# A two-layer relational graph network: gathers of the first six chunks, layer 1's weight sums and the buffers of gathered rows are moved

## The chip, the core and the metric

The kernel runs on one NeuronCore of one Trainium2 chip. The metric is the device time of one execution in microseconds. Before the change it is 22033.58 us, the median of three runs (22026.26, 22033.58, 22033.65). The execution that the profiler recorded took less: 16730.85 us, of which the trace covers 16729.1 us. The page does not say why the two differ; all times of single stages below are times of the recorded execution.

## What is computed

There are 50,000 nodes with 128 features each and 850,000 edges, sorted by the node they point to (`dst`). Each edge has a source node `src` and one of 16 relation types. Two layers run one after the other, the second on the output of the first, and the input is added and normalised at the end:

```python
W = jnp.einsum('rb,bio->rio', w_comp, basis)          # 16 relations from 8 bases, 128x128 each
seg = dst.astype(jnp.int32) * N_REL + rel.astype(jnp.int32)
agg = jax.ops.segment_sum(h[src], seg, num_segments=N_ENT * N_REL)
msg = jnp.einsum('nri,rio->no', agg.reshape(N_ENT, N_REL, -1), W)
out = relu(msg + h @ loop_w + bias)
...
x = _layernorm(x + layer2(layer1(x)), axis=-1)
```

Everything is float32. The costly part of the data movement is `h[src]`: 850,000 rows of 512 bytes per layer, from arbitrary places.

## The kernel before

The edges are cut into tiles of 128, and ten tiles (`K = 10`) make a chunk; there are 665 chunks (`C`) per layer, 1,330 in all. The work has two parts, with a branch between them.

**The part ahead of the branch** (lines 151 to 293) turns the edge list into tables that stay in SBUF: `src` (the row numbers, one column of 128 for each tile), `key` (relation and slot of each edge), `slot`, `dist` and `base_i` (where each chunk's nodes lie). It works in seven batches (line 232). A batch loads `raw` through the SyncE queue (line 240, two buffers), VectorE derives `own` and `rel0` from it (lines 261 to 279), ScalarE casts the row numbers (line 281), TensorE transposes both (line 287), and ScalarE and VectorE copy the results into `src` and `key` (line 288). A batch covers 8 groups of 120 tiles, so the first one holds the row numbers of the first 96 chunks. The last value, `good` (line 293), says whether the edges are sorted closely enough for the fast way. Each engine loads it (line 568) and branches.

**The part behind the branch** is `chunked()` (line 316), unrolled for all chunks of both layers. It begins with `combine(0)`, the weights of layer 1. For each relation, VectorE multiplies one base by a coefficient (line 128) and adds seven more (line 130): 128 instructions of 128x128 for a layer, inputs and output all in SBUF. `combine(1)`, layer 2's weights, stands behind layer 1's chunks in the source. The kernel language's scheduler is free to issue an instruction earlier than it stands in the source where nothing it depends on forbids it.

For each chunk, GpSimd issues ten indirect DMAs (`gather`, line 296), each fetching 128 rows into one slice of a buffer `g` out of the pool `gp`, which has six buffers. VectorE builds `hot`, a one-hot matrix of the ten tiles (line 392). TensorE multiplies each gathered tile by it (line 403), two tiles to a PSUM bank `pa` out of the pool `ps_a` (three banks), and ScalarE copies each bank to `aT` (line 410). `finish` for the chunk before is called behind the first two banks: sixteen matmuls with the weights (line 335), then the sums over shared nodes (lines 347 and 351), the loop term (line 355) and the output (lines 357 to 369).

A gather waits for the buffer it writes, and through the semaphores that the kernel language hands out, for the gather eight before it. The buffer comes free when the ten matmuls of the chunk six before have read it. The scheduler puts the wait for this on the first gather of a chunk only. Where a gather needs two waits, the first becomes a wait instruction of its own on GpSimd's queue: the built program has 1,330 of these for 13,282 gathers.

Two operands of VectorE, `grid` and `apart`, are kept in PSUM (lines 93 to 100), so that `hot` and `shift` each have one input in SBUF.

Of the kernel before, what the change touches and what calls it, by code (L numbers as in the profile page):

```python
# [26 lines left out]
F32 = mybir.dt.float32  # L27
# [4 lines left out]
OP = mybir.AluOpType  # L32
# [4 lines left out]
P = 128  # L37
# [3 lines left out]
K = P // WN  # L41
S = K * WN
G = P // K * K
BATCH = 8
EPS = 1e-5
BANK = 512

# [6 lines left out]
def tile_rgcn_resnorm(  # L54
# [15 lines left out]
    nc = tc.nc  # L70
    N, D = x.shape
    NR, NB = w_comp1.shape
    E = edges.shape[1] // 3
    n_tiles = -(-E // P)
    C = -(-n_tiles // K)
# [8 lines left out]
    consts = ctx.enter_context(tc.tile_pool(name="consts", bufs=1))  # L84
# [36 lines left out]
        BIAS.append(b)  # L121
        W.append(consts.tile([P, NR, D], F32, name=f"w{n}"))

    def combine(n):

        for r in range(NR):
            w = W[n][:, r, :]
            nc.vector.tensor_scalar(w, BASIS[n][:, 0, :], COMP[n][:, r, 0:1], None, op0=OP.mult)
            for b in range(1, NB):
                nc.vector.scalar_tensor_tensor(  # L130
                    w, BASIS[n][:, b, :], COMP[n][:, r, b : b + 1], w, op0=OP.mult, op1=OP.add
                )

    ps_a = ctx.enter_context(tc.tile_pool(name="ps_a", bufs=3, space=PSUM))
    ps_o = ctx.enter_context(tc.tile_pool(name="ps_o", bufs=1, space=PSUM))
    ps_n = ctx.enter_context(tc.tile_pool(name="ps_n", bufs=1, space=PSUM))

    def turned(h, m, sb):

# [6 lines left out]
    def column(j, first, ap):  # L146

        return bass.AP(tensor=edges.tensor, offset=edges.offset + j * E + first, ap=ap)


    n_groups = -(-n_tiles // G)
# [7 lines left out]
    with tc.tile_pool(name="meta1", bufs=1) as m1, tc.tile_pool(name="meta", bufs=2) as mp:  # L159
# [34 lines left out]
        for c0 in range(0, C, D):  # L194
            cs = slice(c0, min(c0 + D, C))
            k = cs.stop - c0
# [35 lines left out]
        for i in range(n_batches):  # L232
            g0 = i * BATCH
            q = min(BATCH, n_groups - g0)
            t0 = g0 * G
            raw = mp.tile([P, 3, BATCH, P], I32, name="raw")
            whole = min(q, (E // P - t0) // G)
            for j in range(3):
                if whole:
                    nc.sync.dma_start(  # L240
                        raw[:G, j, :whole, :], column(j, t0 * P, [[P, G], [G * P, whole], [1, P]])
                    )
            if whole < q:

                nc.vector.memset(raw[:, 0, whole, :], 0)
                nc.vector.memset(raw[:, 1, whole, :], N)
                nc.vector.memset(raw[:, 2, whole, :], NR)
                t1 = t0 + whole * G
                n_whole, n_rest = divmod(E - t1 * P, P)
                for j in range(3):  # L250
                    if n_whole:
                        nc.sync.dma_start(
                            raw[:n_whole, j, whole, :], column(j, t1 * P, [[P, n_whole], [1, P]])
                        )
                    if n_rest:
                        nc.sync.dma_start(
                            raw[n_whole : n_whole + 1, j, whole, :n_rest],
                            column(j, (t1 + n_whole) * P, [[n_rest, 1], [1, n_rest]]),
                        )
            tb = mp.tile([P, BATCH], F32, name="tb")  # L260
            nc.vector.tensor_scalar(tb[:G, :q], raw[:G, 1, :q, 0], float(N - WN), None, op0=OP.min)
            rel0 = mp.tile([P, BATCH, P], F32, name="rel0")
            nc.vector.tensor_tensor(  # L263
                rel0[:G, :q], raw[:G, 1, :q, :], tb[:G, :q, None].to_broadcast([G, q, P]), op=OP.subtract
            )
            own = mp.tile([P, BATCH, P], F32, name="own")
            nc.vector.tensor_scalar(own[:G, :q], rel0[:G, :q], 0.0, None, op0=OP.is_ge)
            nc.vector.scalar_tensor_tensor(
                own[:G, :q].rearrange("p g e -> p (g e)"),
                rel0[:G, :q].rearrange("p g e -> p (g e)"),  # L270
                float(WN),
                own[:G, :q].rearrange("p g e -> p (g e)"),
                op0=OP.is_lt,
                op1=OP.mult,
                accum_out=picked[:G, i : i + 1],
            )
            nc.vector.scalar_tensor_tensor(  # L277
                rel0[:G, :q], raw[:G, 2, :q, :], float(WN), rel0[:G, :q], op0=OP.mult, op1=OP.add
            )
            srcf = mp.tile([P, BATCH, P], F32, name="srcf")  # L280
            nc.scalar.copy(srcf[:G, :q], raw[:G, 0, :q, :])
            for of, to, engine in ((srcf, src, nc.scalar.copy), (rel0, key, nc.vector.tensor_copy)):
                for h0 in range(0, q, BANK // P):
                    h = min(BANK // P, q - h0)
                    tp = ps_a.tile([P, BANK], F32, name="pa")
                    for j in range(h):
                        nc.tensor.transpose(tp[:, j * G : (j + 1) * G], of[:G, h0 + j, :], ident[:G, :G])  # L287
                    engine(to[:, (g0 + h0) * G : (g0 + h0 + h) * G], tp[:, : h * G])
        pick = m1.tile([P, 1], F32, name="pick")
        nc.vector.tensor_reduce(pick, picked, AX.X, OP.add)  # L290
        total = ps_o.tile([P, D], F32, name="po")
        nc.tensor.matmul(total[:1, :1], pick, ones[:, 0:1], start=True, stop=True)
        nc.vector.tensor_scalar(good, total[:1, :1], float(E + C + S * C), None, op0=OP.is_equal)

    def gather(to, of, idx):
        nc.gpsimd.indirect_dma_start(  # L296
            out=to, out_offset=None, in_=of, in_offset=bass.IndirectOffsetOnAxis(ap=idx, axis=0)
        )

    def normed(t, m, sb):  # L300

# [12 lines left out]
        return o  # L314

    def chunked():
        combine(0)
        with tc.tile_pool(name="gp", bufs=6) as gp, tc.tile_pool(name="hp", bufs=2) as hp, tc.tile_pool(
            name="sb", bufs=3
        ) as sb:  # L320

# [49 lines left out]
            for n, of in enumerate((x, H1)):  # L371
                kept, late = None, None

                def finish(kept, c, k, aT, hw, n0, xw):
                    kept, a = nodes_of(c, k, slots(c, k, aT, n), kept, hw, n)
                    ended(n, a, n0, xw)
                    return kept

                for c in range(C):
                    ks = min(K, n_tiles - c * K)  # L380
                    n0 = at(c)
                    hw = sb.tile([P, D], F32, name="hw")
                    nc.sync.dma_start(hw, of[ds(n0, P), :])
                    xw = None
                    if n:
                        xw = sb.tile([P, D], F32, name="xw")
                        nc.sync.dma_start(xw, x[ds(n0, P), :])
                    g = gp.tile([P, K, D], F32, name="g")
                    for k in range(ks):
                        gather(g[:, k, :], of, src[:, c * K + k : c * K + k + 1])  # L390
                    hot = hp.tile([P, K, NR * WN], F32, name="hot")
                    nc.vector.tensor_tensor(  # L392
                        hot[:, :ks],
                        grid[:, None, :].to_broadcast([P, ks, NR * WN]),
                        key[:, c * K : c * K + ks, None].to_broadcast([P, ks, NR * WN]),
                        op=OP.is_equal,
                    )
                    aT = hp.tile([P, NR, S], F32, name="aT")
                    for k in range(0, ks, 2):
                        m = min(2, ks - k)  # L400
                        pa = ps_a.tile([P, BANK], F32, name="pa")
                        for i in range(m):
                            nc.tensor.matmul(  # L403
                                pa[:, i * NR * WN : (i + 1) * NR * WN],
                                g[:, k + i, :],
                                hot[:, k + i, :],
                                start=True,
                                stop=True,
                            )
                        nc.scalar.copy(  # L410
                            aT[:, :, k * WN : (k + m) * WN].rearrange("p r (i w) -> p i r w", w=WN),
                            pa[:, : m * NR * WN].rearrange("p (i r w) -> p i r w", i=m, w=WN),
                        )
                        if k == 2 and late is not None:
                            kept = finish(kept, *late)
                            late = None
                    if late is not None:
                        kept = finish(kept, *late)
                    late = c, ks, aT, hw, n0, xw
                finish(kept, *late)  # L420
                if n == 0:
                    combine(1)
# [189 lines left out]
```

## Time and profile before

| | busy us | share of the span | instructions |
|---|---|---|---|
| TensorE matmul (PE) | 13415.4 | 80% | 78570 |
| TensorE weight load (PEld) | 11315.1 | 68% | 78570 |
| VectorE (DVE) | 5048.0 | 30% | 10325 |
| ScalarE (ACT) | 4657.3 | 28% | 12650 |
| GpSimd (POOL) | 12558.5 | 75% | 13290 |

[...] Between two gathers the trace shows 0.30 us in which it is not busy and waits for nothing that the profile names ("issue"); a share of 75% can therefore be a queue without any hole in it. [...] The packets of all DMA queues together take 24% of the sixteen engines' time. The mean clock granted to TensorE is 0.89; its records switch between full and half.

### The profile page before, as it was taken

The numbers are of one execution on the slowest core, as the hardware profiler recorded it, in microseconds if no ns is written. First come the engines' busy times: TensorE is split into PE (matmuls) and PEld (weight loads), VectorE is DVE, ScalarE is ACT, GpSimd is POOL, SyncE is SP. The second block draws the span as 40 slices with busy tenths as digits, with TensorE's granted clock in tenths as the row PEclk, the third lists the DMA queues.
The fourth block names the chain that finished last, engine by engine and source line by source line (L and its number), as shares of the span: only waits on it lengthen the run. The fifth ranks groups of instructions, "written<-read, shape, count | busy, mean of one in ns | idle before, by whom it ended". The sixth has DMA issues, their size and how long they took to land.

```text
span 16729.1 us, 222138 instructions
## 1 busy us (share of the span) xinstructions
PE 13415.4 (80%) x78570; PEld 11315.1 (68%) x78570; DVE 5048.0 (30%) x10325; ACT 4657.3 (28%) x12650; POOL 12558.5 (75%) x13290
## 2 busy tenths in 40 slices
PE   6888888878888888888888888888878888888787
PEld 5666666666666666666666666666666666666666
DVE  4222222222222222222233333333333333333333
ACT  2222222222222222222223222222222222222222
POOL 6777777777777777777777777777777777777777
PEclk9888888888888888888888889898888888888888
DMA  3222222222222222222222222222222222222222
GB/s 75 64 64 64 64 64 64 64 64 64 64 64 64 64 64 64 64 64 64 64 66 69 69 69 69 69 69 69 69 69 69 69 69 69 69 69 69 69 69 66
DMA packets 934787, 1115.38 MB, mean 67 GB/s; under 512 B 272843, under 2 KB 721179, under 8 KB 933691
## 3 DMA queue, kind: packets, MB, share of 16 engines
q0 software_dynamic: 425024, 871.30, 18.4%
q1 hardware_dynamic: 505723, 228.35, 4.9%
q8 instruction: 649, 10.63, 0.3%
q14 instruction: 447, 3.66, 0.1%
q10 hardware_dynamic: 2944, 1.44, 0.0%
HBM read 1012.86 MB, written 87.16 MB: 66 GB/s over the span
## 4 chain that ended last, share of the span: by engine, by line
POOL 41%; PE 26%; DMA 17%; issue 16%; DVE 0%; POOLq 0%; ACT 0%; SPq 0%; DVEq 0%; ACTq 0%
POOL g L296 41%; PE ps L335 16%; DMA g<-H,src 8%; DMA g<-in_x_dram,src 8%; PE pa L403 6%; PE pn L347 1%; PE pn L351 1%; PE po L355 1%; PE po L141 0%; DMA raw<-in_edges_dram 0%; DMA first_i<-in_edges_dram 0%; POOLq L296 0%; PE pa L287 0%; DVE rel L263 0%; DVE rel L277 0%
## 5 line engine op out<-in xcount | busy, mean ns | idle before, releaser
L403 PE MATMUL pa<-hot,g 128*128 128x192 f32 x26564 | 6758.5, 367 | 3246.0 <-DMA g<-in_x_dram,src 1430.2
L296 POOL DMA_INDIRECT g<-in_x_dram,src x6641 | 6291.7, 947 | 2109.0 <-issue 1782.5
L296 POOL DMA_INDIRECT g<-H,src x6641 | 6265.8, 944 | 2039.9 <-issue 1781.9
L403 PEld LDWEIGHTS pa<-hot,g 128*128 128x128 f32 x26564 | 4307.9, 199 | 5052.1 <-ACT aT L410 1885.8
L335 PEld LDWEIGHTS ps<-w,aT 128*120 128x120 f32 x42560 | 6078.3, 221 | 2.1 <-ACT aT L410 0.8
L335 PE MATMUL ps<-w,aT 128*120 128x128 f32 x42560 | 6021.0, 311 | 0.2
L410 ACT COPY aT<-pa 128x384 f32<-128x384 f32 x6642 | 3173.9, 478 | 6146.0 <-PE pa L403 6144.3
L350 DVE TENSOR_SCALAR shift<-apart,dist 128x128 f32<-128x128 f32 x1328 | 466.0, 351 | 10148.7 <-PE pn L351 10148.7
L392 DVE TENSOR_TENSOR hot<-grid,key 128x1920 f32<-128x1920 f32 x1330 | 2866.0, 2155 | 1244.1 <-PE pa L403 1233.9
L337 ACT COPY slots<-ps 120x128 f32<-120x128 f32 x1330 | 353.9, 266 | 4871.6 <-PE ps L335 4871.6
L347 PE MATMUL pn<-slots,own 120*128 120x128 f32 x2660 | 649.2, 326 | 0.4
L353 ACT COPY kept<-pn 128x128 f32<-128x128 f32 x1330 | 353.8, 266 | 841.1 <-PE pn L351 841.1
L347 PEld LDWEIGHTS pn<-slots,own 120*128 120x128 f32 x2660 | 395.5, 187 | 283.3 <-ACT slots L337 283.3
L355 PE MATMUL po<-loop,hT 128*128 128x128 f32 x2660 | 515.0, 275 | 0.4 <-ACT hT L143 0.4
L351 PE MATMUL pn<-kept,shift 128*128 128x128 f32 x2656 | 513.2, 274 | 0.0
L343 DVE TENSOR_SCALAR own<-grid,slot 120x128 f32<-120x128 f32 x1330 | 448.5, 337 | 0.0
L358 DVE TENSOR_TENSOR pn<-pn,s 128x128 f32<-128x128 f32 x1330 | 399.1, 300 | 150.7 <-ACT kept L353 9.3
L355 PEld LDWEIGHTS po<-loop,hT 128*128 128x128 f32 x2660 | 403.3, 192 | 0.7 <-ACT hT L143 0.7
L351 PEld LDWEIGHTS pn<-kept,shift 128*128 128x128 f32 x2656 | 402.8, 191 | 0.2
L357 DVE TENSOR_TENSOR s<-po,bias 128x128 f32<-128x128 f32 x1330 | 373.8, 281 | 17.9 <-PE po L355 17.8
L141 PE MATMUL po<-ident,hw 128*128 128x128 f32 x1330 | 363.0, 273 | 8.9 <-DMA hw<-H 4.7
L143 ACT COPY hT<-po 128x128 f32<-128x128 f32 x1330 | 360.7, 271 | 12.5 <-DVE w L130 8.4
(72 smaller groups left out, 1817.3 us busy)
## 6 DMA issues: line engine op xcount, KB each, us to landing
g<-in_x_dram,src POOLq DMA_INDIRECT x6641
g<-H,src POOLq DMA_INDIRECT x6641
hw<-in_x_dram SPq DMA_DIRECT2D x665, 64.0 KB
H<-h SPq DMA_DIRECT2D x665, 64.0 KB
hw<-H SPq DMA_DIRECT2D x665, 64.0 KB
xw<-in_x_dram SPq DMA_DIRECT2D x665, 64.0 KB
out_dram<-o SPq DMA_DIRECT2D x665, 64.0 KB
raw<-in_edges_dram SPq DMA_DIRECT2D x18, 480.0 KB
```

What stands on the lines that cost most here:

```text
L296: nc.gpsimd.indirect_dma_start(out=to, out_offset=None, in_=of, in_offset=bass.IndirectOffsetOnAxis(ap=idx, axis=0))
L335: nc.tensor.matmul(ps[: k * WN], aT[:, r, : k * WN], W[n][:, r, :], start=r == 0, stop=r == NR - 1)
L343: nc.vector.tensor_scalar(own[: k * WN], grid[: k * WN, :P], slot[: k * WN, c : c + 1], None, op0=OP.is_equal)
L347: nc.tensor.matmul(pn, own[: k * WN], st[: k * WN], start=True, stop=not c)
L350: nc.vector.tensor_scalar(shift, apart, dist[:, c - 1 : c], None, op0=OP.is_equal)
L351: nc.tensor.matmul(pn, shift, kept, start=False, stop=True)
L355: nc.tensor.matmul(po, turned(hw, P, sb), LOOP[n], start=True, stop=True)
L357: nc.vector.tensor_add(s, po, BIAS[n])
L358: nc.vector.tensor_add(pn, pn, s)
L392: nc.vector.tensor_tensor(hot[:, :ks], grid[:, None, :].to_broadcast([P, ks, NR * WN]), key[:, c * K : c * K + ks, None].to_broadcast([P, ...
L403: nc.tensor.matmul(pa[:, i * NR * WN : (i + 1) * NR * WN], g[:, k + i, :], hot[:, k + i, :], start=True, stop=True,)
L410: nc.scalar.copy(aT[:, :, k * WN : (k + m) * WN].rearrange("p r (i w) -> p i r w", w=WN), pa[:, : m * NR * WN].rearrange("p (i r w) -> p i ...
```

## The change

It has three parts. The gathers of the first six chunks of layer 1 are issued in the part ahead of the branch, as soon as the first batch has their row numbers, so that GpSimd, which has nothing to do there, works while VectorE finishes the tables. For that the rows need buffers that outlive both parts: six fixed tiles take the place of the pool. The weights of layer 1 also go ahead of the branch, into the first batch, and each weight is summed in a PSUM bank and copied to SBUF by ScalarE, four relations at a time; so an addition has one input in SBUF in place of two. Layer 2's weights take the same form at their old place in the source. The banks come from `ps_a`, which both parts use.

```diff
+GATHERS = 6
...
+    def combine(n):
+
+        for r0 in range(0, NR, BANK // D):
+            pa = ps_a.tile([P, BANK], F32, name="pa")
+            for r in range(r0, r0 + BANK // D):
+                w = pa[:, (r - r0) * D : (r - r0 + 1) * D]
+                nc.vector.tensor_scalar(w, BASIS[n][:, 0, :], COMP[n][:, r, 0:1], None, op0=OP.mult)
+                for b in range(1, NB):
+                    nc.vector.scalar_tensor_tensor(
+                        w, BASIS[n][:, b, :], COMP[n][:, r, b : b + 1], w, op0=OP.mult, op1=OP.add
+                    )
+            nc.scalar.copy(W[n][:, r0 : r0 + BANK // D, :].rearrange("p r d -> p (r d)"), pa)
...
+    rows = [consts.tile([P, K, D], F32, name=f"g{i}") for i in range(GATHERS)]
+    n_first = 0
...
+            if not i:
+                combine(0)
...
+            while n_first < min(GATHERS, C - 1) and (n_first + 1) * K <= (g0 + q) * G:
+                for k in range(K):
+                    gather(rows[n_first][:, k, :], x, src[:, n_first * K + k : n_first * K + k + 1])
+                n_first += 1
...
     def chunked():
-        combine(0)
-        with tc.tile_pool(name="gp", bufs=6) as gp, tc.tile_pool(name="hp", bufs=2) as hp, tc.tile_pool(
+        with tc.tile_pool(name="hp", bufs=2) as hp, tc.tile_pool(
...
-                    g = gp.tile([P, K, D], F32, name="g")
-                    for k in range(ks):
+                    g = rows[(n * C + c) % GATHERS]
+                    for k in range(ks if n or c >= n_first else 0):
                         gather(g[:, k, :], of, src[:, c * K + k : c * K + k + 1])
```

More of the change, by code (lines that the diff above doesn't have):

```diff
@@ L122, in tile_rgcn_resnorm @@
         W.append(consts.tile([P, NR, D], F32, name=f"w{n}"))
[L124 to L132, printed above, removed]
     ps_a = ctx.enter_context(tc.tile_pool(name="ps_a", bufs=3, space=PSUM))
@@ L136, in tile_rgcn_resnorm, with gather @@
     ps_n = ctx.enter_context(tc.tile_pool(name="ps_n", bufs=1, space=PSUM))
+    def combine(n):
[9 more added lines that the diff above has]
+            nc.scalar.copy(W[n][:, r0 : r0 + BANK // D, :].rearrange("p r d -> p (r d)"), pa)
+    def gather(to, of, idx):
+        nc.gpsimd.indirect_dma_start(
+            out=to, out_offset=None, in_=of, in_offset=bass.IndirectOffsetOnAxis(ap=idx, axis=0)
+        )
     def turned(h, m, sb):
@@ L293, in tile_rgcn_resnorm @@
         nc.vector.tensor_scalar(good, total[:1, :1], float(E + C + S * C), None, op0=OP.is_equal)
[L295 to L298, printed above, removed]
     def normed(t, m, sb):
```

## Prediction

> **What bounds the kernel now.** I read first the chain of work that ended last and the costliest groups on the page.
>
> ```profile
> POOL 41%; PE 26%; DMA 17%; issue 16%; DVE 0%; POOLq 0%; ACT 0%; SPq 0%; DVEq 0%; ACTq 0%
> ...
> L296 POOL DMA_INDIRECT g<-in_x_dram,src x6641 | 6291.7, 947 | 2109.0 <-issue 1782.5
> L296 POOL DMA_INDIRECT g<-H,src x6641 | 6265.8, 944 | 2039.9 <-issue 1781.9
> ```
>
> GpSimd's gathers lead the chain, and most of their idle time is "issue", which no engine ends. The timeline of a stretch in the middle shows the queue:
>
> ```profile
> 3012.81 0.95 POOL L296 DMA_INDIRECT g<-in_x_dram,src  x1 [0.30 <-issue]
> ...
> 3014.06 0.94 POOL L296 DMA_INDIRECT g<-in_x_dram,src  x1 [0.30 <-DMA g<-in_x_dram,src]
> ```
>
> A gather starts every 1.25 us (0.944 busy, 0.30 between), whatever the releaser named. Over the whole trace the starts are 1.248 us apart on average; 13,282 x 1.248 = 16,580 us of the 16,729. So the recorded execution is one GpSimd queue without holes, about 150 us of start and layer change aside. The start is where the change works, so I read it next: windows by stage, then the timeline behind the branch.
>
> ```profile
> core 0: us, PE busy (x) PEld busy (x) DVE busy (x) ACT busy (x) POOL busy (x), PEclk, DMA share, GB/s
> ...
> 20.00:32.00 12.00, 6.87 (x27) 5.02 (x27) 8.78 (x22) 4.85 (x6) 0.00 (x0) 1.00 1.12 195
> 32.00:50.00 18.00, 12.88 (x45) 9.23 (x46) 13.75 (x28) 3.67 (x5) 0.00 (x0) 1.00 0.85 154
> 50.00:85.80 35.80, 15.35 (x71) 12.73 (x69) 25.79 (x43) 7.51 (x11) 0.00 (x0) 1.00 0.67 121
> 85.80:118.40 32.60, 1.24 (x3) 0.68 (x3) 32.60 (x129) 0.27 (x1) 28.94 (x9) 1.00 0.08 24
> ```
>
> Ahead of the branch GpSimd does nothing, and VectorE is busy 8.78 + 13.75 + 25.79 = 48.3 of 65.8 us. Behind it VectorE is full for 32.6 us with the 128 additions of `combine(0)` and the first instruction after them, and GpSimd makes nine gathers in that time, where its pace elsewhere would make 26.
>
> ```profile
> 87.03 1.27 POOL L296 DMA_INDIRECT g<-in_x_dram,src  x1 [85.44 <-DVE w L130]
> 88.60 2.24 POOL L296 DMA_INDIRECT g<-in_x_dram,src  x1 [0.30 <-issue]
> 91.15 3.77 POOL L296 DMA_INDIRECT g<-in_x_dram,src  x1 [0.30 <-issue]
> ...
> 118.35 4.21 DVE L392 TENSOR_TENSOR hot<-grid,key 128x1920 f32<-128x1920 f32 x2
> 119.54 0.94 POOL L296 DMA_INDIRECT g<-in_x_dram,src  x1 [0.30 <-issue]
> ...
> 120.74 7.72 PE L403 MATMUL pa<-hot,g 128*128 128x192 f32 x28 [30.46 <-DMA g<-in_x_dram,src]
> ```
>
> Gathers take up to 3.77 us beside the additions and 0.94 again at 119.54, once `hot` (which reads PSUM) has replaced them. Until then the queue has done 9 gathers, 11.2 us of work at 1.248: it stands as if it had started undisturbed at 119.54 - 11.2 = **108.3 us**. TensorE's first chunk starts at 120.74, behind `hot`.
>
> The timed runs take 22,034 us, 5,303 more than the recorded execution, and no view says where. If it is the gathers, one costs 1.248 + 5303/13,282 = 1.65 us there; it could as well be TensorE, whose clock the records show at half in places.
>
> [...]
>
> **The change, part by part.**
>
> *Gathers ahead of the branch.* They need the first batch's `src`, which ScalarE writes at 28.62 us (two casts, 1.02 us); only `ident`, raw data and a `pa` bank stand ahead of that. I take 30 us for the first gather, against 87.03: **57.0 us** earlier. Both ends: 28 us if nothing moves, 45 if four of `combine(0)`'s banks hold up the transposes or the casts.
>
> *No two-SBUF additions beside the gathers.* Nine gathers took 119.54 - 87.03 = 32.5 us in place of 11.2: **21.3 us** given back, if the PSUM form doesn't disturb[...].
>
> *New disturbance.* The sixty early gathers now run beside the tables. A batch has L263 (1.23 us), L267 (0.68), L268 (1.22), L277 (1.22) = 4.35 us of VectorE work with two SBUF operands or SBUF to SBUF; six batches lie after 30 us, 26 us in all. Behind the branch GpSimd lost 21.3 of 32.6 us, a share of 0.65, so I charge 0.65 x 26 = **17 us**; ends 0 and 26.
>
> *The branch moves back.* VectorE gets 128 more instructions ahead of it. They start 0.254 us apart in before (32.6/128); [...] 33 to 41 us in all. VectorE has 65.8 - 48.3 = 17.5 us free there, and the data waits of lines 240 and 261 leave part of it usable. The branch comes at 85 + 33 - 17 = 101 at best, 85 + 41 = 126 at worst; I take 112. Queued behind it are `hot` and TensorE's first chunk, at 112 + 3.5 = 115.5. GpSimd is not: its sixty gathers last until 30 + 60 x 1.248 + 17 = 122. Its next gather needs the first matmul of chunk 0, done by then. With the branch at 126 it waits about 8 us.
>
> *Sum for GpSimd*: 57 + 21.3 - 17, less 3 for a chance of the last wait = **58 us**.
>
> *Fixed buffers.* The pool gave one wait for TensorE per chunk. With fixed tiles each gather overwrites a slice that one matmul has read, so I expect a wait on each, and a wait instruction on nearly every gather, some 12,000 more. In the trace's records such an instruction takes 17 ns, and a gather behind one starts 1.249 us (median) after the one before, as without one (1.249). [...] I charge 0. Upper end, if they came on top: 12,000 x 17 ns = 204 us. The waits are long fulfilled: TensorE reads a buffer within one chunk, and five lie between.
>
> *Layer 2's weights in PSUM*: four banks borrowed from `ps_a` in turn, in VectorE's free time (30% busy). TensorE keeps two banks meanwhile, and the steady chunk doesn't change. 0. *Layer change*: GpSimd waits 16.3 us for H in both. 0.
>
> **Rivals.** (1) *GpSimd's queue sets the time in the timed runs too*, or the extra 5.3 ms lie outside: 22,034 - 58 = **21,976**; if the start is stretched with the rest, 58 x 1.317 = 76, 21,958. For it: the chain. Chance 0.52. (2) *TensorE sets it in the timed runs*: its start alone counts, 120.7 against 115.5 (105 to 130): **22,028**. For it: half clock records and 80% busy; against: at 109 ns a pass of L335 at full clock and 213 at half, a chunk's 59 passes (L403's twenty of 192 columns taken in proportion) fill 14.7 us even at half clock, under the 16.5 that a chunk takes in the timed runs (22,034 less 100 at the start, over 1,330). Chance 0.20. (3) *The added wait instructions count*, because the timed queue is bound by its sequencer: 21,976 + 204 = **22,180**, slower. Against: the 1.249 us on both sides. Chance 0.15. (4) *The early gathers are held up* [...]: start at 45, 26 us lost, 10 us waiting: 57 + 21.3 - 15 - 26 - 10 = 27 us, **22,007**. Chance 0.13.
>
> **How the numbers follow.** Case 1 gives the time, 21,976. A difference of 0.2% is 44 us. Faster: most of case 1, and the better ends of 2 and 4, 0.58. Within: 0.13 from case 2, 0.06 from case 4, 0.06 from weak ends of 1 and 3, 0.25. Slower: case 3 and the bad end of 2, 0.17. The range runs from 21,935, below case 1 stretched, to 22,100, half of the wait instructions' bound; it leaves out most of case 3.
>
> **What would show it.** Right: gathers from about 30 us, sixty of them by 122, at 0.94 us wherever VectorE adds in PSUM; the branch between 101 and 126; gathers 1.249 us apart in the middle; a recorded span near 16,729 - 58 = 16,671. Wrong: a pace other than 1.249 (case 3), a queue that stands still at the branch (case 4), or a recorded span that falls by 58 while the timed runs stay (case 2).

## The result, and the profile after

| | kernel before | changed kernel |
|---|---|---|
| device time, median | 22029.92 us (4 runs, 22017.26 to 22033.65) | 21105.69 us (4 runs, 21104.94 to 21115.74) |
| ratio, 95% interval | | 0.9582, 0.9566 to 0.9599 |

The change saves 924 us where 58 were forecast. One thing has to be said first, because no number below can be understood without it: the kernel before, unchanged, took 16,730 to 16,736 us in some sets of runs and 21,378 to 22,195 us in others (medians), all runs of a set alike, and two of the chips showed both; the recorded execution on the page of before is of the first kind, its timed runs are of the second. I call them the **short** and the **long pace**. The page of the changed kernel is of the long pace.

Page of the changed kernel: the chain by engine, then three of the costliest groups (busy us, mean ns | idle us before, and what ended most of it).

```profile
another core or an unknown queue 51%; PE 35%; DVE 6%; ACT 5%; issue 3%; DMA 0%; ACTq 0%; DVEq 0%; SPq 0%
...
L143 POOL DMA_INDIRECT g<-H,src x6641 | 6280.8, 946 | 4256.8 <-remote 1456.9
L143 POOL DMA_INDIRECT g<-in_x_dram,src x6641 | 6288.2, 947 | 4213.2 <-PE pa L416 1452.7
...
L350 ACT COPY slots<-ps 120x128 f32<-120x128 f32 x1330 | 353.9, 266 | 10860.0 <-remote 10744.5
```

GpSimd led the chain of before with 41% and is not in this one at all. A gather costs what it did, 0.946 us, but GpSimd's idle time before gathers is 8,470 us instead of 4,149: the queue has holes now, 3.2 us in each of the 1,330 chunks. The copy of `slots`, which waits for the sixteen matmuls that sum a chunk (each shows as two passes, so x32 below), waits 10,860 us instead of 4,872, and for something without a name ("remote"). The same copy in before's recorded execution, on its page and in its timeline:

```profile
L337 ACT COPY slots<-ps 120x128 f32<-120x128 f32 x1330 | 353.9, 266 | 4871.6 <-PE ps L335 4871.6
```

```profile
3003.28 3.66 PE L335 MATMUL ps<-w,aT 128*120 128x128 f32 x32
...
3006.97 0.27 ACT L337 COPY slots<-ps 120x128 f32<-120x128 f32 x1 [3.01 <-PE ps L335]
```

The timeline of one chunk of the changed kernel:

```profile
3001.95 3.66 PE L348 MATMUL ps<-w,aT 128*120 128x128 f32 x32
...
3005.44 0.27 PE L150 MATMUL po<-ident,hw 128*128 128x128 f32 x1
...
3008.28 0.95 POOL L143 DMA_INDIRECT g<-in_x_dram,src  x1 [0.30 <-issue]
3011.13 0.27 ACT L350 COPY slots<-ps 120x128 f32<-120x128 f32 x1 [8.50 <-remote]
...
3011.45 0.95 POOL L143 DMA_INDIRECT g<-in_x_dram,src  x1 [2.22 <-remote]
3011.45 0.50 PEld L360 LDWEIGHTS pn<-slots,own 120*128 120x128 f32 x2 [5.70 <-ACT slots L350]
```

The matmuls are over at 3005.6. The copy that needs nothing but them starts at 3011.13. TensorE's semaphore records have no update between 3001.80 and 3011.11, and then three within 80 ns. So the work was done, and the news of it, the update for which the copy waits, came 5.5 us late. By then GpSimd had stopped, since its next gather also waits for TensorE. This is so in nearly every chunk: the copy starts 5.9 us (median) after the recorded end of the matmuls, and in before's recorded execution 0.037 us.

Page groups and timeline of the same kernel at the short pace (a later run, 16,681 us):

```profile
L143 POOL DMA_INDIRECT g<-in_x_dram,src x6641 | 6273.4, 945 | 2077.0 <-issue 1191.3
L143 POOL DMA_INDIRECT g<-H,src x6641 | 6265.9, 944 | 2039.3 <-issue 1215.4
```

```profile
3003.69 5.27 PE L348 MATMUL ps<-w,aT 128*120 128x128 f32 x32
...
3008.35 0.94 POOL L143 DMA_INDIRECT g<-in_x_dram,src  x1 [0.30 <-issue]
...
3009.00 0.27 ACT L350 COPY slots<-ps 120x128 f32<-120x128 f32 x1 [4.59 <-PE ps L348]
```

There the copy starts 0.04 us after the matmuls, and GpSimd has no holes: 4,116 us of idle time, 0.31 for each of 13,282 gathers. The difference of the two executions, 21,103 - 16,677 = 4,426 us, is GpSimd's added idle time, 8,470 - 4,116 = 4,354, but for 30 us that the gathers themselves took longer and 42 us more between the last gather and the end.

### The profile page after: what moved, and what is told of

Same layout as the page of the kernel before. It is cut to its first block, busy times and chain, and to the rows that moved or that the text cites. A ratio compares the mean times of both kernels' runs of the same rounds, so it can differ in the third digit from the quotient of the medians.

```text
span 21102.8 us, 234031 instructions
## 1 busy us (share of the span) xinstructions
PE 13307.9 (63%) x78570; PEld 12874.7 (61%) x78570; DVE 5172.9 (25%) x10325; ACT 4703.9 (22%) x12658; POOL 12570.0 (60%) x13290
## 4 chain that ended last, share of the span: by engine, by line
another core or an unknown queue 51%; PE 35%; DVE 6%; ACT 5%; issue 3%; DMA 0%; ACTq 0%; DVEq 0%; SPq 0%
PE pa L416 23%; PE pn L360 5%; DVE hot L405 5%; PE po L368 3%; PE pn L364 3%; ACT aT L423 2%; ACT slots L350 2%; ACT o L327 1%; PE ps L348 1%; DVE pa L137 0%; DVE own L356 0%; DVE rs L323 0%; DMA raw<-in_edges_dram 0%; DMA first_i<-in_edges_dram 0%
## 5 line engine op out<-in xcount | busy, mean ns | idle before, releaser
L416 PEld LDWEIGHTS pa<-hot,g 128*128 128x128 f32 x26564 | 6378.9, 267 | 177.4 <-issue 96.0
L360 PE MATMUL pn<-slots,own 120*128 120x128 f32 x2660 | 1035.0, 492 | 7479.6 <-ACT slots L350 7366.6
L360 PEld LDWEIGHTS pn<-slots,own 120*128 120x128 f32 x2660 | 649.0, 303 | 7873.2 <-ACT slots L350 7751.5
L348 PE MATMUL ps<-w,aT 128*120 128x128 f32 x42560 | 4903.1, 274 | 46.6 <-issue 45.1
L348 PEld LDWEIGHTS ps<-w,aT 128*120 128x120 f32 x42560 | 4850.8, 184 | 55.8 <-issue 50.1
L368 PE MATMUL po<-loop,hT 128*128 128x128 f32 x2660 | 832.4, 416 | 5.0 <-issue 3.7
L364 PE MATMUL pn<-kept,shift 128*128 128x128 f32 x2656 | 829.6, 415 | 0.0
L368 PEld LDWEIGHTS po<-loop,hT 128*128 128x128 f32 x2660 | 713.9, 327 | 7.2 <-issue 5.1
L364 PEld LDWEIGHTS pn<-kept,shift 128*128 128x128 f32 x2656 | 713.0, 327 | 0.2
L327 ACT ACTIVATE o<-t,nm,rs 128x128 f32<-128x128 f32 x665 | 327.7, 493 | 413.1 <-DVE nm L325 153.5
```

Source lines behind the costliest of these rows:

```text
L327: nc.scalar.activation(o[:m], t, AF.Identity, bias=nm[:m], scale=rs[:m])
L348: nc.tensor.matmul(ps[: k * WN], aT[:, r, : k * WN], W[n][:, r, :], start=r == 0, stop=r == NR - 1)
L360: nc.tensor.matmul(pn, own[: k * WN], st[: k * WN], start=True, stop=not c)
L364: nc.tensor.matmul(pn, shift, kept, start=False, stop=True)
L368: nc.tensor.matmul(po, turned(hw, P, sb), LOOP[n], start=True, stop=True)
L416: nc.tensor.matmul(pa[:, i * NR * WN : (i + 1) * NR * WN], g[:, k + i, :], hot[:, k + i, :], start=True, stop=True,)
```

## Experiments

The expectations say what their letters stand for; e4 uses A and B for a question of its own. In the others they are: **A**: the fixed buffers carry the gain, since GpSimd may refill a slice as soon as one matmul has read it. Rivals of it: the start (C) or the weights in PSUM (D) carry it. And on what the long pace is: **T**, gathers hold up the semaphore updates of the other engines, whoever waits for whom; **U**, it takes the loop in which GpSimd and TensorE wait for each other; **W**, GpSimd's waiting itself does it; **V**, TensorE is slow there.

### The kernel before again (e1), and the fixed buffers alone (e2)

```diff
-        with tc.tile_pool(name="gp", bufs=6) as gp, ...
+        rows = [consts.tile([P, K, D], F32, name=f"g{i}") for i in range(GATHERS)]
...
-                    g = gp.tile([P, K, D], F32, name="g")
+                    g = rows[(n * C + c) % GATHERS]
```

> The kernel before, unchanged, to have a profile of it at the pace of its timed runs. Theory A (GpSimd and TensorE wait for each other in a loop: with the pool, GpSimd may refill a buffer only when TensorE has done a whole chunk): about 22,030 us, a chunk every 16.5 us, GpSimd waiting for TensorE about 4 us in each chunk, TensorE standing still in one place of each chunk for 5 us or more, and at half clock after it. Rival B (a gather is slower in the timed runs): about 22,030 us, no holes in GpSimd's queue, each gather 1.65 us instead of 1.248.

> The kernel before with the six fixed row buffers in place of the pool, nothing else changed: no early gathers, the weights made in SBUF behind the branch. Theory A (the release of a buffer slice by slice carries the gain): 21,105 + 60 to 80 for the start that it lacks = 21,165 to 21,185 us, a ratio of 0.961. Rival C (the start or the phase in which the early gathers put the two queues carries it): 22,030 us, ratio 1.000. Rival D (the weights summed in PSUM carry it): 22,030 us.

Measured: 16,734.81 us for the kernel before as a run of its own, and 16,735.36 for the fixed buffers beside before's 16,735.55 (17 runs): ratio 1.0000 (0.9992 to 1.0008). The set fell on the short pace, which none of the theories had foreseen. So the pace is not the program's, and at the short pace the fixed buffers are worth nothing, as the prediction had charged them.

### The changed kernel again (e4), and with the pool put back (e5)

The pool serves every chunk from the seventh on; the first six keep the fixed buffers that their early gathers fill. A first form (e3), with the pool opened ahead of the branch for the early gathers too, gave no time: its waits deadlock.

```diff
-                    g = rows[(n * C + c) % GATHERS]
+                    g = rows[c] if not n and c < n_first else gp.tile([P, K, D], F32, name="g")
```

> The changed kernel, unchanged, beside the kernel before. The two earlier comparisons showed the kernel before at two paces: 22,030 us beside the changed kernel's 21,105, and 16,735 us in a later set. Theory A (the pace belongs to the chip or its moment, not to the program; where before runs at 16,735, GpSimd's queue sets the time and the prediction's sum holds): 16,735 - 58 = 16,677 us, ratio 0.9965; where before runs at 22,030: 21,105, ratio 0.958. Rival B (the changed kernel keeps 15.8 us per chunk wherever it runs): 21,105 us in both, which is a ratio of 1.26 beside 16,735.

> The changed kernel with the pool of six buffers for every chunk after the first six (those keep the fixed buffers that their early gathers fill): early gathers and weights in PSUM stay, from chunk 6 on GpSimd waits once per chunk again. Where before runs at 16,735 us: theory A 16,677 us, as the changed kernel, ratio 0.9965. Where before runs at 22,030 us: if the release slice by slice carries the gain, 21,970 us, ratio 0.997; if the start carries it, 21,105 us, ratio 0.958.

This set was at the long pace, before at 22,194.65 us. Changed kernel 21,146.65, ratio 0.9526 (0.951 to 0.9542). With the pool 22,185.41, ratio 0.9995 (0.9986 to 1.0004). With the pool the gain is gone, though early gathers and weights in PSUM are there: C and D fall. This is also the price of those two parts at the long pace: 22,194.65 - 22,185.41 = 9 us, at most 31 by the interval, where the prediction had 58. Groups of the kernel with the pool:

```profile
L143 POOL DMA_INDIRECT g<-H,src x6641 | 6264.7, 943 | 5054.3 <-PE pa L416 2865.7
L143 POOL DMA_INDIRECT g<-in_x_dram,src x6641 | 6271.5, 944 | 4532.9 <-PE pa L416 1840.1
```

GpSimd idles 9,587 us before its gathers here, 1,072 more than in the recorded execution of the changed kernel of the same set (8,515); the two spans differ by 22,182.4 - 21,144.5 = 1,038. That is nearly the whole gain of this set, 22,194.65 - 21,146.65 = 1,048. How it comes about is in the holes: counting the gathers between two holes of over 0.5 us, the kernel with the pool stops once in a chunk, after exactly ten gathers, for 3.4 us (median; 2.5 to 7.5 from the 5th to the 95th percentile), 4.13 us a chunk beyond the usual 0.30. With fixed buffers it stops twice, after nine gathers and after one, for 2.1 us each (median), 3.33 a chunk. (4.13 - 3.33) x 1,330 = 1,064 us. So the buffers carry the gain, and the stops show where it lies; that two short stops cost less because the release comes slice by slice is argued from them and was not shown apart from the other things that fixed tiles change.

### Fixed buffers alone at the long pace (e9, e13)

> The kernel before with fixed row buffers alone, again, for a chip on which before runs at 22 ms: if the release slice by slice carries the gain there, a ratio of 0.953 to 0.962 (changed kernel 0.953 and 0.958, and 60 us for the start that it lacks). If the buffers need the early start beside them: 1.00. Where before runs at 16.7 ms: 1.000, as in the first such run.

> The kernel before with fixed row buffers alone, for a chip on which before runs at 22 ms: if the release slice by slice carries the gain there, a ratio of 0.953 to 0.962; if it needs the early start beside it, 1.00. Where before runs at 16.7 ms: 1.000, as twice before.

The first of these met the short pace once more: 16,730.47 beside 16,730.60, ratio 0.9999 (0.9989 to 1.001). The second met the long one: 20,953.51 us beside 21,377.93, ratio 0.9810 (0.9769 to 0.9851). These are two runs against three, and the interval stays below 1: faster without any early start, so A holds in kind. GpSimd stops twice in a chunk here too, after nine gathers and after one, for 1.9 us. In size I missed: the time of the fixed buffers is near that of the changed kernel in the other sets (20,954 against 21,106 and 21,147), but before took 21,378 here, 650 to 820 us less than in the two other comparisons. At the long pace the kernel with the pool is not one number.

### Where the pace comes from: gathers taken apart (e6 to e8, e10, e11)

Three kernels leave parts of the computation out. In the first every gather goes to a spare buffer; in the second a plain transfer of 128 consecutive rows takes the place of each; in the third 14 of 16 relations are left out of the sums.

```diff
-                        gather(g[:, k, :], of, src[:, c * K + k : c * K + k + 1])
+                        gather(junk[:, k, :], of, src[:, c * K + k : c * K + k + 1])
```

```diff
+    def straight(to, of, i):
+        n0 = i * P % (N - P)
+        nc.sync.dma_start(to, of[n0 : n0 + P, :])
...
-                        gather(g[:, k, :], of, src[:, c * K + k : c * K + k + 1])
+                        straight(g[:, k, :], of, c * K + k)
```

```diff
-                for r in range(NR):
+                for r in (0, NR - 1):
```

> The changed kernel, all gathers into a spare buffer that nobody reads; TensorE multiplies rows that are set to 0.5 once at the start (so the gathered rows are left out of the result). GpSimd never waits for TensorE, nor TensorE for a gather. Where before runs at 16.7 ms, all theories: 16,650 to 16,700 us, GpSimd's queue alone, TensorE 9.5 us a chunk. Where it runs at 22 ms: theory T (the gathers hold up TensorE's semaphore updates, whoever waits for whom): TensorE takes 16 us or more a chunk as long as gathers run, and 9.5 after they end near 16,650 us; in all about 19,000 to 22,000 us, updates up to 8 us late. Rival U (the two only wait for each other in a loop through the buffers): 16,650 to 16,700 us, updates within 20 ns. Rival V (TensorE itself is slow on such a chip): 15 us a chunk to the end, about 20,000 us, no change when the gathers end.

> The changed kernel, each gather replaced by one plain transfer of 128 consecutive rows on SyncE's queue: the same bytes into the same buffers, behind the same waits, but wrong rows, so the indices are left out of the computation. Where before runs at 22 ms: theory T with GpSimd's part in it [...]: no update late, TensorE sets the time, about 9.5 us a chunk, 12,700 us. Theory T with the transfers themselves (any write into SBUF with its semaphore updates): updates late, 15 us a chunk, 19,000 to 21,000 us. Rival V: 20,000 us. Where before runs at 16.7 ms: 12,700 us in all.

> The changed kernel with 2 of the 16 relations in the group of matmuls that sums a chunk (14 are left out): 28 passes, 3.05 us of TensorE less in each chunk. Where before runs at 22 ms: theory T: the time stays within 2% of the changed kernel's 21,105 to 21,147 us, since a chunk is ten gathers (12.5 us) and the stops in which updates come through (3.3 us). Rival V (the group itself takes 9 us there): the chunk falls to GpSimd's 12.5 us, 16,700 us. Where before runs at 16.7 ms: 16,677 us.

> The kernel of the spare buffer again (all gathers into a buffer that nobody reads, TensorE multiplies rows of 0.5), for a chip on which before runs at 22 ms; where before ran at 16,731 it took 16,664 us. Theory T (gathers hold up TensorE's semaphore updates, whoever waits for whom): TensorE takes 16 us or more a chunk while gathers run, less after they end near 16,650 us; in all 19,000 to 22,000 us. Rival U (only the loop of waits through the buffers): 16,664 us, updates within 20 ns. Rival V (TensorE is slow on such a chip): 15 us a chunk to the end, 20,000 us.

> The changed kernel again, for a chip on which before runs at 16,731 us. There GpSimd's queue sets the time and the prediction's sum should hold: 16,731 - 58 = 16,673 us, ratio 0.9965. Rival B (the changed kernel keeps 15.8 us per chunk wherever it runs): 21,105 us. Where before runs at 22 ms: 21,105 to 21,147 us, as before.

All met the short pace (before at 16,730.60 and 16,730.18), where they tell less, but not nothing. Without gathers (second kernel) 10,411.57 us, 7.8 us a chunk: that is what TensorE alone needs, less than the 12,700 I had put. The spare buffer took 16,664.09 and 16,663.08, the lighter sums 16,672.30: GpSimd's queue alone. The changed kernel itself took 16,681.00 beside 16,730.18, ratio 0.9969 (0.9956 to 0.9983): the forecast of 58 us was a forecast for this pace, and 49 came. So its 15.8 us a chunk belong to the moment, as theory A of e4 has it, and not to the kernel.

### All conditions in one run (e12, e14, e17 to e19)

Since no run could be made to meet the long pace, I put twelve conditions of 111 chunks into one kernel, so that one run compares them; in most of them gathers or sums are left out. There are two such kernels; the edit picks by layer and stage (cut out of the second):

```diff
+                    stage = n, c // STAGE
+                    order = range(ks if n or c >= n_first else 0)
...
+                    if stage in ((0, 4), (1, 2)):
+                        order = order[:8]
```

> Twelve stages of 111 chunks (the last of each layer 110) in one run, so that all are measured on the same chip; rows are wrong or left out in most of them, as said. Layer 1: A the changed kernel; B its gathers in reverse order of the slices, so that the first one waits for the last matmul of the chunk six before, as the pool made it; C all gathers into a spare buffer, TensorE multiplies old rows; D plain transfers of consecutive rows on SyncE's queue; E no gathers; F three buffers instead of six. Layer 2: G the changed kernel; H one slice of ten gathered; I five of ten; J 2 of 16 relations in the summing group; K plain transfers of consecutive rows on GpSimd's queue; L the sums of the chunk before taken up after slice 6 instead of slice 2. Where before runs at 16.7 ms, all theories: 12.5 us a chunk wherever ten gathers are made, 7.8 to 9.5 elsewhere, every update within 20 ns. Where it runs at 22 ms: theory T (gathers hold up TensorE's semaphore updates): A, F, G, J 15.8, B 16.5, C 16 or more until the gathers end, D, E 7.8 to 9.5, H 8 to 10, I 10 to 13, K as G if the software queue is enough for it and 8 to 10 if the indices are needed, L 14 to 16. Rival U (only the loop of waits): as T, but C 9.5. Rival V (TensorE is slow there): D and E 14 or more, J 12.5.

> Again twelve stages of 111 chunks (the last of each layer 110) in one run; rows are wrong or left out in some, as said. Layer 1: A all gathers into a spare buffer, ahead of all others on GpSimd's queue, TensorE multiplies rows of 0.5 (in the earlier staged run these gathers had slipped into the stages before theirs); B the changed kernel; C its gathers in reverse order of the slices, so that the first waits for the last matmul of the chunk six before, as with the pool; D six of ten slices gathered; E eight of ten; F the changed kernel. Layer 2: G the changed kernel; H reverse order; I eight of ten; J the sums of the chunk before taken up after slice 8; K 2 of 16 relations in the summing group; L the changed kernel. Where before runs at 21 to 22 ms: theory T (gathers hold up TensorE's semaphore updates, whoever waits for whom): A 12 us a chunk or more as long as its gathers run (1,390 us), with updates over 1 us late, and 7.7 after; B, F, G, L 15.4 to 15.8; C, H 16.3 to 16.8; D 8.5 to 10; E 11 to 13; J 15.2; K 12.5 to 14. Rival U (it takes the loop of waits between the two): the same, but A 7.7 us a chunk from the start and no update late. Rival W (GpSimd's waiting for TensorE's semaphore itself holds up that semaphore): A 7.7, and C, H below B, since they wait ten times less often. Where before runs at 16.7 ms: 12.5 us wherever ten gathers are made, 10.0 with eight, 7.7 in A and D.

The first (e12) met the long pace at once (before at 21,377.93); the second at its fourth run (e19; before at 21,405.78), after three at the short pace (e14, e17, e18), 15,581 us each.

> The second staged run again, for a chip or a moment at which before runs at 21 to 22 ms; where it ran at 16.7 ms, the stages ran at GpSimd's pace. Expected as before: theory T (gathers hold up TensorE's semaphore updates, whoever waits for whom): A 12 us a chunk or more as long as its gathers run (1,390 us), with updates over 1 us late, and 7.7 after; B, F, G, L 15.4 to 15.8; C, H 16.3 to 16.8; D 8.5 to 10; E 11 to 13; J 15.2; K 12.5 to 14. Rival U (it takes the loop of waits between the two): the same, but A 7.7 us a chunk from the start and no update late. Rival W (GpSimd's waiting for TensorE's semaphore holds that semaphore up): A 7.7, and C, H below B.

> The second staged run a third time, for a moment at which before runs at 21 to 22 ms. The early gathers of the changed kernel, which wait for nobody, already made TensorE's updates late in such runs (half or more of them by over 0.1 us between 50 and 130 us, none before the first gather), so theory T (gathers hold up the updates, whoever waits for whom) is now expected to hold: A 12 us a chunk or more while its gathers run, with updates over 1 us late, 7.7 after; B, F, G, L 15.4 to 15.8; C, H 16.3 to 16.8 if the whole-chunk wait is what costs the kernel before its extra time, 15.4 to 15.8 if it is not; D 8.5 to 10; E and I 11 to 13; J 15.2; K 12.5 to 14. Where before runs at 16.7 ms: as in the two runs before.

> The second staged run a last time, for a moment at which before runs at 21 to 22 ms. Theory T (gathers hold up TensorE's semaphore updates, whoever waits for whom): A 12 us a chunk or more while its gathers run, with updates over 1 us late, 7.7 after; B, F, G, L 15.4 to 15.8; C, H 16.3 to 16.8 if the whole-chunk wait is what costs the kernel before its extra time, 15.4 to 15.8 if it is not; D 8.5 to 10; E and I 11 to 13; J 15.2; K 12.5 to 14. Where before runs at 16.7 ms: as in the three runs before.

Times of a chunk, from the starts of the `slots` copies in each stage. "Late" is the share of TensorE's updates that the trace shows over 1 us after the end of their matmul (some semaphore records are missing at the long pace, so a little of it may be lost, not late). The last chunks of a stage already run beside the gathers of the next, which lifts the means of the light stages a little: the median chunk takes 7.71 us in e12 E and K.

| stage | short pace (e14), us | long pace, us | late |
|---|---|---|---|
| ten gathers, changed kernel (e19 B, G, L; e12 G) | 12.46, 12.47, 12.48 | 15.52, 15.70, 15.26; 15.37 | 23 to 26% |
| three buffers (e12 F) | | 15.32 | 26% |
| eight gathers (e19 E, I) | 9.85, 9.99 | 12.33, 12.49 | 30 to 32% |
| six gathers (e19 D) | 7.71 | 9.39 | 29% |
| every other slice, five (e12 I) | | 8.36 | 2% |
| one gather (e12 H) | | 7.72 | 0 |
| none (e12 E) | | 7.79 | 1% |
| plain transfers, SyncE (e12 D) | | 7.71 | 0 |
| plain transfers, GpSimd's queue (e12 K) | | 8.03 | 1% |
| lighter sums (e12 J; e19 K) | 12.47 | 14.00; 14.34 | 39 to 40% |
| sums taken up later (e12 L; e19 J) | 12.48 | 15.22; 15.69 | 26 to 27% |
| reverse order (e19 C, H) | 12.50, 12.47 | 15.15, 15.56 | 26 to 27% |
| ten gathers that nobody waits for (e19 A) | 7.71 | 165.2 | see below |

V falls: without gathers TensorE takes 7.7 us a chunk at the long pace too, at full clock. The plain transfers bring the same bytes into the same buffers behind the same waits, in less time, and make nothing late. It takes the gathers, and about six of them a chunk: five, expected to take 10 to 13 us, made little late. Whether the indices do it, or a queue of GpSimd that hardly pauses, isn't told apart: six gathers of 1.25 us fill 7.5 of TensorE's 7.7 us, while the ten plain transfers from its queue (K, below) keep GpSimd busy for 558 us of 820. Windows of the first staged kernel at the long pace: its stages D, G and K.

```profile
core 0: us, PE busy (x) PEld busy (x) DVE busy (x) ACT busy (x) POOL busy (x), PEclk, DMA share, GB/s
...
5800.00:6590.00 790.00, 790.00 (x6049) 768.25 (x6048) 335.32 (x512) 334.27 (x921) 0.00 (x0) 1.00 0.36 101
...
9340.00:10920.00 1580.00, 1015.70 (x6003) 982.33 (x6003) 433.08 (x1019) 384.14 (x1019) 938.03 (x995) 0.81 0.21 55
...
14330.00:15150.00 820.00, 799.35 (x6070) 776.68 (x6070) 428.42 (x1030) 386.91 (x1028) 558.26 (x1028) 0.99 0.39 108
```

D and K move 101 and 108 GB/s, and TensorE is idle for at most 3% of the time; G moves 55, and TensorE is busy for 64%.

The stage of gathers that nobody waits for decides between T, U and W. Its window at the short pace (e14) while its gathers run, and then two at the long pace (e19), while they run and after them; the columns are those above:

```profile
300.00:950.00 650.00, 650.00 (x4980) 632.15 (x4979) 274.43 (x422) 273.89 (x756) 491.50 (x521) 1.00 0.27 71
```

```profile
300.00:1600.00 1300.00, 133.90 (x445) 107.76 (x444) 24.46 (x38) 26.02 (x70) 996.88 (x936) 0.52 0.18 48
1610.00:2360.00 750.00, 734.02 (x5560) 712.14 (x5560) 308.31 (x472) 307.92 (x848) 0.00 (x0) 0.98 0.06 18
```

At the short pace TensorE makes its 59 passes in 7.71 us, with the same gathers beside it. At the long pace TensorE makes 445 passes in 1,300 us: a chunk takes 165.2 us, chunk after chunk, and 7.71 as soon as the last of these gathers is out. I had expected 12 us or more. GpSimd waits for TensorE nowhere in it (3 wait instructions to 936 gathers), so U and W fall and T holds. The timeline shows that not only updates are held up:

```profile
789.18 0.18 PEld L352 LDWEIGHTS ps<-w,aT 128*120 128x120 f32 x1 [1.06 <-issue]
...
790.57 0.27 PE L352 MATMUL ps<-w,aT 128*120 128x128 f32 x1 [2.26 <-issue]
791.28 0.28 PEld L352 LDWEIGHTS ps<-w,aT 128*120 128x120 f32 x1 [1.92 <-issue]
...
792.68 0.37 PE L352 MATMUL ps<-w,aT 128*120 128x128 f32 x1 [1.83 <-issue]
```

Weight loads and matmuls, which need no semaphore here, follow each other at multiples of about 0.7 us, one or two to a gather, where the stage at the short pace has one every 0.11. The same is seen in the changed kernel: its sixty early gathers wait for nobody but `src`, and at the long pace half and more of TensorE's updates between 50 and 130 us are over 0.1 us late (none before the first gather), against 1 of 30 at the short pace.

Two stages told less than they should. Reverse order was to give a chunk the pool's single wait, but the scheduler sorted the gathers again and left 7.1 waits to ten gathers, where the changed kernel has 9.9 and the pool one; its times don't bear on A. And in the first staged kernel the gathers of its stage C had slipped in between those of A and B, fifteen a chunk; their 22.16 and 20.78 us a chunk aren't used.

### The early start, beside the fixed buffers (e15, e16)

> The changed kernel beside the fixed buffers alone, on one chip. Where before runs at 21 to 22 ms: 21,000 to 21,150 us; the early start, worth 49 us in the set with before at 16,730, should make it 49 us faster than the fixed buffers alone, if the start still counts there; no difference if TensorE's late updates set the pace from the first chunk on. Where before runs at 16.7 ms: 16,681 us, ratio 0.997.

> The kernel before with fixed row buffers alone, beside the changed kernel. Where before runs at 21 to 22 ms: 20,950 to 21,200 us, 49 us slower than the changed kernel, if the start counts there. Where before runs at 16.7 ms: 16,730 us.

Short pace, before at 16,731.36: changed kernel 16,682.01 (ratio 0.997, 0.9958 to 0.9983), fixed buffers alone 16,732.89 (1.0001, 0.9991 to 1.0011). The start and the PSUM weights are worth 51 us there, as expected. For the long pace the two were not measured beside each other; there the pool's run (e5) left them 9 us.

### What stays open

Why an execution has one pace or the other. It isn't the program and it isn't the chip alone. One lead: at the long pace the trace lacks semaphore records (16,192 updates of TensorE recorded for 18,750 instructions that make one, against 18,703 at the short pace). Whether the missing records and the instructions that issue a few at a time have one cause, and whether the recording is part of it, no run here tells, as none leaves the records out. Nor did any experiment give a kernel that beats the changed one at both paces: at the short pace the ten gathers of a chunk are the bound, at the long one the same gathers and the stops between them.

## Why the prediction was wrong

**The step that failed** is the one from the recorded execution to the timed runs. The prediction noted that the timed runs take 5,303 us more and that no view says where, and then charged each part of the change by the recorded execution. For that execution it was nearly right: a recorded span near 16,671 us was forecast for the changed kernel, and at the short pace it was 16,677. The term that was mis-sized is *Fixed buffers*, charged 0: it is 0 at the short pace (ratios 1.0000, 0.9999, 1.0001), and at the long pace it measured 22,185.41 - 21,146.65 = 1,039 us in one set and, alone, 424 in another. The reason given, "the waits are long fulfilled: TensorE reads a buffer within one chunk, and five lie between", holds where TensorE's updates arrive in 14 ns and fails where a quarter of them come over 1 us late. That the direction was right is luck: the gain was forecast from the start, and the start gave 9 us at the pace of the timed runs.

**Rivals.** The first took the extra time for the gathers, 1.65 us each: a gather takes 0.946 at the long pace as well, and the time is in the holes. The second, that TensorE sets the timed runs, named the engine whose news is late, for another reason; its refutation, 14.7 us of passes at half clock against 16.5, was sound, since what is missing isn't TensorE's work. The third, that the added wait instructions cost up to 204 us, is refuted by the same ratios of 1.0000. The fourth, early gathers held up, came true in kind at the short pace, with 49 us against its 27. Two readings were a little off and change none of this: over the whole trace of before the gathers start 1.249 us apart in the median and 1.251 on average, not 1.248, and 13,282 x 1.248 is 16,576.

**The start, point by point**, by the run of the changed kernel at the short pace. Timeline of it:

```profile
53.00 1.06 PE L302 MATMUL pa<-ident,srcf 120*128 120x120 f32 x4 [14.90 <-ACT w L140]
54.10 0.56 ACT L303 CAST src<-pa 128x480 int32<-128x480 f32 x1 [1.15 <-PE pa L302]
...
54.94 1.09 POOL L143 DMA_INDIRECT g<-in_x_dram,src  x1 [53.35 <-ACT src L303]
...
58.69 2.14 DVE L137 SCALAR_TENSOR_TENSOR pa<-basis,comp,pa 128x128 f32<-128x128 f32 x8
...
60.09 0.94 POOL L143 DMA_INDIRECT g<-in_x_dram,src  x1 [0.30 <-issue]
...
65.29 1.21 DVE L283 SCALAR_TENSOR_TENSOR own<-rel,own 120x1024 f32<-120x1024 f32 x1
65.53 1.78 POOL L143 DMA_INDIRECT g<-in_x_dram,src  x1 [0.30 <-issue]
...
126.11 4.22 DVE L405 TENSOR_TENSOR hot<-grid,key 128x1920 f32<-128x1920 f32 x2 [0.93 <-DVE good L312]
```

- *First gather at 30 us*: it came at 54.94. The transposes stood 14.9 us behind the copy of a weight bank; the banks of `ps_a` are lent to `combine(0)`. That is worse than the bad end of 45. Against before's 89.15 in its new run it is 34.2 us, not 57.
- *21.3 us given back*: before's first sixty gathers took 95.6 us from first to last start in place of 59 x 1.248 = 73.6, so 21.9 were there to be had. Right.
- *No disturbance by PSUM additions*, an assumption of the prediction: the five gathers from 56.34 to 61.33 took 0.94 to 0.95 beside them, and only the first, at 54.94, took 1.09. Right.
- *17 us of new disturbance*: sixty gathers took 136.06 - 54.94 = 81.1, so 7.5. The instructions of lines 278 to 292 do slow gathers, 1.78 beside line 283 above, but they cost 7.5 of the 26 us that VectorE spends on them, a share of 0.29 and not the 0.65 charged.
- *3 us of waiting behind the branch*: none; the next gather follows in 1.25 us, at 137.31. Sum: 34.2 + 21.9 - 7.5 = 48.6; measured 49 and 51.
- *The branch at 112*: `hot` started at 126.11, the worst end. An addition in PSUM started 0.257 us after the one before (eight in 2.14, the last taking 0.34), against 0.262 in SBUF in before (median of additions that follow each other). The upper end of the 33 to 41 us forecast for the 128 instructions was my estimate, and no view of before showed it; 128 x 0.257 is 33. The additions cost VectorE no more; they only stood in the way. It hurt nobody, as foreseen: the sixty gathers last until 137.

## What to carry to other kernels

When timed runs and the recorded execution differ by more than the measurement, the profile at hand may not describe what is timed: ask for an execution at the timed pace, or forecast for both, before any step is charged. What a wait that is "long fulfilled" costs hung here on how prompt the semaphores were: giving each consumer its own release, slice by slice, cost nothing where updates came 14 ns after the matmul and saved 2 to 5% where about a quarter of them came over 1 us after it. And a resource borrowed from a pool that the critical load also uses, as the three banks were, can delay that load: here the transposes stood 14.9 us behind the copy of a bank, and the first gather came 25 us later than the 30 expected.

## What the hardware showed that I had not expected

The same program on the same chip took 16,730 us in one set and 21,378 in another. At the longer pace indirect gathers, one every 1.25 to 1.4 us, go with other engines held up: about a quarter of the updates of TensorE's semaphore arrived over 1 us after the matmul instead of 14 ns, those of a chunk's sums 5 to 6 us, and beside gathers that waited for nobody a chunk took 165.2 us in place of 7.71, a factor of 21. Plain transfers of the same bytes, from SyncE's or GpSimd's queue, at twice the rate, did not. And where TensorE's passes were cut by 28 of 59, a chunk at the longer pace fell only from 15.37 to 14.00 us.
